# A two-layer graph network on one core: another order of the seven products of each block multiplication, of GpSimd's work and of the matrix M, and another prologue

## The chip, the cores and the metric

The kernel runs on one core of a Trainium2 chip. The core has five engines that run their own instruction queues side by side: TensorE (PE in the profile, its weight loads PEld), VectorE (DVE), ScalarE (ACT), GpSimd (POOL) and SyncE (SP), which here issues all DMA transfers. The metric is the device time of one execution in microseconds (us), lower is better. Three runs of the kernel before gave 2621.05, 2624.15 and 2624.7 us; the median is 2624.15 us.

## The reference

There are 128 graphs of 128 nodes, with x of 128x128x512 and an adjacency of 128x128x128, all float32. Two layers follow each other, each behind a layer norm and a relu and each added to its input. Cut to what matters:

```
# layer 0
h = maximum(layernorm(x), 0)
A_hat = adj + eye;  d = A_hat.sum(-1) ** -0.5
x = x + (A_hat * d[:, :, None] * d[:, None, :]) @ (h @ W0 + b0)

# layer 1
h  = maximum(layernorm(x), 0)
H  = (adj != 0);  Dn = 1 / (H @ adj[:, 0, :]);  Be = 1 / H.sum(axis=1)
conv(z, W, b) = Dn * (H @ (Be * (H^T @ (z @ W^T)))) + b
r  = layernorm(relu(conv(h, W1, b1))) * gamma + beta     # 1024 wide
x  = x + conv(r, W2, b2)
```

## The kernel before, in words

Two graphs form a pair, two pairs a group of four graphs. There are 64 pairs and 32 groups. The weights stay in SBUF. For each group the kernel forms, from the adjacency, the transposed matrix for layer 0 (`aT`), H transposed (`hT`), the same scaled by Be (`hb`, L237, on GpSimd) and M = H Be H^T (`m`, four 128-wide products at L245 in `adj_M`), so that layer 1 needs one product with M per convolution.

**Three block multiplications per pair.** The products with W0 (`s_w0`), W1 (`s_w1`) and W2 (`s_w2`) go through `strassen` (L342 on): rows are split by the two graphs of the pair, columns and the inner size in halves, so that seven products of blocks stand where eight would be. The products are called after their left and right blocks: 11·11, 12·21, s1·t1, s2·t2, s3·t3, 22·t4, s4·22. The left sums s1 to s4 are made in `left_sums` (L331 to L334, four GpSimd instructions in a chain) for W0 and W2, in `left_matmul` (L278 to L281) for W1. The right sums t1 to t4 are made once per weight in `Weight.sums` (L81). Results leave PSUM through VectorE or ScalarE, and two of the seven combinations per multiplication run on GpSimd (L376, u4, and L379).

**The stages.** The work is a software pipeline written out by hand (`tc.manual_schedule()`): the instructions of an engine run in the order in which the program gives them. In stage t, TensorE does W1 of pair t, then, if t is even, M of the next group, then W2 of pair t-1, W0 of pair t+2, and then four short things: the last product with M (`s_kv`, L519), the two products with M ahead of W1 (`s_mhT`, L458), the product with `aT` (`s_lap`, L422), and, if t is odd, the four transposes of `adj_T` (L220). There are 65 stages, t = 0 to 64.

**Filling.** Work of VectorE that is not tied to a product (statistics, edges, normalisation) stands in a list, `fill`, with a cost for each item. After each product `fill.give` adds the spare time of that product to an account and emits items from the front of the list while the account covers them; `fill.all` empties the list. A GpSimd instruction that an item emits takes its place in GpSimd's queue at that moment.

**The chain of pair t in its stage.** W1's result `r` is scaled and shifted (`first`, L478, one 128x1024 instruction per graph, i = 1 and then 0), put through relu on ScalarE (L481), its statistics are taken (`second`, L484 and L486), `chain` (L160 to L170) makes 1/std and the shift out of them, `norm2` (L499, two GpSimd instructions) applies them, and `turn` (L287) transposes 32x32 blocks on VectorE. At the stage's end `s_zT` issues 16 transfers (L324) that finish the transposition, into the tile `na`, the left blocks of W2 in the next stage. The same holds for pair t+3 and W0: `start` (L394) makes `h0` from x, `turn` follows, and `s_h0T` issues 16 transfers into `la`. The tile `r` has one buffer, so that the next stage's W1 can write its result only once the 16 transfers have read it.

The order in stage t is

```
W1 of t with left_sums(na of t-1) ahead of it; base(t); stats_r, statistics -> list
left_sums(la of t+2);  [t even: adj_M];  W2 of t-1;  W0 of t+2;  fill.all()
s_zT(t);  s_h0T(t+3);  s_kv(t-1);  s_mhT(t+1);  s_lap(t+2);  [t odd: adj_T, loads]
```

`base` (L449 and L450) is four GpSimd additions that add b2 and the layer's input to the tile into which the result goes.

Of the kernel before, what the change touches and what calls it, by code (L numbers as in the profile page):

```python
# [14 lines left out]
P = 128  # L15
# [5 lines left out]
def adj_preln_kernel(  # L21
# [41 lines left out]
    class Weight:  # L63
# [11 lines left out]
        def sums(self, *which):  # L75

            b = self.b
            for k in which or range(4):
                t, x, y = (("t1", "12", "11"), ("t3", "22", "12"), ("t2", "22", "t1"), ("t4", "t2", "21"))[k]
                eng = nc.gpsimd if k == 3 else nc.vector  # L80
                eng.tensor_tensor(b[t], b[x], b[y], ALU.subtract)  # L81

    wt0 = Weight("w0", NF // 2, F // 2)
# [39 lines left out]
    def load_group(g):  # L123
        gs = slice(g * G, (g + 1) * G)
        a4 = load.tile([P, G, P], F32, tag="a4", name="a4")
        w4 = load.tile([P, G, P], F32, tag="w4", name="w4")
        x4 = load.tile([P, G, F], F32, tag="x4", name="x4")
        xs = x[gs].rearrange("g i f -> i g f")
        if g == 0:

            nc.sync.dma_start(x4[:, 0, :], xs[:, 0, :])
            nc.sync.dma_start(x4[:, 1, :], xs[:, 1, :])
            nc.sync.dma_start(a4, adj[gs].rearrange("g i j -> i g j"))
            nc.sync.dma_start(x4[:, 2, :], xs[:, 2, :])
            nc.sync.dma_start(x4[:, 3, :], xs[:, 3, :])
            weight0()
            nc.sync.dma_start(w4, adj[gs, 0, :].partition_broadcast(P))
        else:
            nc.sync.dma_start(a4, adj[gs].rearrange("g i j -> i g j"))
            nc.sync.dma_start(w4, adj[gs, 0, :].partition_broadcast(P))  # L140
            nc.sync.dma_start(x4, xs)
        groups[g] = {"x": x4, "a": a4, "w": w4}

# [68 lines left out]
    def adj_T(g):  # L214

        q = groups[g]
        a4, d = q["a"], q["d"]
        tr = psum.tile([P, G, P], F32, tag="ps", name="tr")
        for k in range(G):
            nc.tensor.transpose(tr[:, k, :], a4[:, k, :], ident)  # L220
        aT = prep.tile([P, G, P], F32, tag="aT", name="aT")
        nc.vector.tensor_tensor(
            aT, tr, ident.unsqueeze(1).to_broadcast([P, G, P]), ALU.add
        )
        hT = prep.tile([P, G, P], F32, tag="hT", name="hT", bufs=1)
        nc.vector.tensor_scalar(hT, tr, 0.0, None, ALU.not_equal)
        nc.gpsimd.tensor_tensor(aT, aT, d.unsqueeze(2).to_broadcast([P, G, P]), ALU.mult)
        bi = small.tile([P, G], F32, tag="bi", name="bi")
        hb = prep.tile([P, G, P], F32, tag="hb", name="hb", bufs=1)
        q.update(aT=aT, hT=hT, hb=hb)  # L230

        def first():

            nc.vector.tensor_reduce(bi, hT, AX.X, ALU.add)
            nc.vector.tensor_scalar_max(bi, bi, 1.0)
            nc.vector.reciprocal(bi, bi)
            nc.gpsimd.tensor_tensor(hb, hT, bi.unsqueeze(2).to_broadcast([P, G, P]), ALU.mult)  # L237

        fill.add(1000, first)
# [105 lines left out]
    def strassen(a, wt, tag, dst, bias=None):  # L345


        h = wt.half

        def tmp(n):  # L350
            return work.tile([P, h], F32, tag=n, name=tag + n, bufs=1)


        pe, add = wt.nk * h * 1.68, 70 + h * 1.21

        def taken(n, ps, k):
            t = tmp(n)
            if bias is None:
                nc.scalar.copy(t, ps)
                fill.give(pe)  # L360
            else:
                nc.vector.tensor_tensor(t, ps, bias[:, k, :], ALU.add)
                fill.give(pe - add)
            return t

        def summed(t, a, b, op=ALU.add):
            nc.vector.tensor_tensor(t, a, b, op)  # L367
            return t

        u1 = taken("u1", product(a, wt, "11", "11"), 0)  # L370
        summed(dst[0][0], product(a, wt, "12", "21"), u1)
        fill.give(pe - add)
        u5 = taken("u5", product(a, wt, "s1", "t1"), 1)
        u2 = summed(tmp("u2"), product(a, wt, "s2", "t2"), u1)
        u4 = tmp("u4")
        nc.gpsimd.tensor_tensor(u4, u2, u5, ALU.add)  # L376
        fill.give(pe - add)
        u3 = summed(tmp("u3"), product(a, wt, "s3", "t3"), u2)
        nc.gpsimd.tensor_tensor(dst[1][1], u3, u5, ALU.add)  # L379
        fill.give(pe - add)  # L380
        summed(dst[1][0], u3, product(a, wt, "22", "t4"), ALU.subtract)
        fill.give(pe - add)
        summed(dst[0][1], product(a, wt, "s4", "22"), u4)
        fill.give(pe - add)

    def start(t):

        c = pairs[t] = {}
        c["q"], c["k"] = groups[t // 2], (t % 2) * 2
        q = c["q"]  # L390
        h = work.tile([P, 2, F], F32, tag="h0", name="h0", bufs=1)
        for i in range(2):
            k = c["k"] + i
            nc.scalar.activation(  # L394
                h[:, i, :], q["x"][:, k, :], AF.Relu,
                bias=q["nb"][:, k : k + 1], scale=q["s"][:, k : k + 1],
            )
        c["h0"] = h

        if t > 2:  # L400
            for i in range(2):
                fill.add(610, turn, h[:, i, :])
# [67 lines left out]
    def stats_r(mv, t):  # L470
# [15 lines left out]
                nc.vector.bn_aggr(mv[:, R + i, :], st[:, i].rearrange("p j s -> p (j s)"))  # L486

        for i in (1, 0):
            fill.add(1290, first, i)
        for i in (1, 0):  # L490
            fill.add(680, second, i, 0)
            fill.add(880, second, i, 1)
# [68 lines left out]
    def weight1():  # L561

        rows = [w[:, n, :] for w in s["w1"] for n in range(w.shape[1])]
        for r, w in enumerate(rows):
# [4 lines left out]
            for k in range(2):  # L569
# [1 line left out]
                    wt1.b[f"{k + 1}{j + 1}"][:, :, n * P : (n + 1) * P],  # L571
                    ps[:, 2 * k : 2 * k + 2, :],
                )
        wt1.sums()

    def weight2():

        rows = [w[:, n, :] for w in s["w2"] for n in range(w.shape[1])]
        for r, w in enumerate(rows):
            j, n = divmod(r, NF // 2)  # L580
            for k in range(2):
# [4 lines left out]
                for c in range(4):  # L586
                    nc.tensor.transpose(ps[:, c, :], wk[:, c // 2, c % 2], ident)
                nc.scalar.copy(wt2.b[f"{k + 1}{j + 1}"][:, :, n * P : (n + 1) * P], ps)
        bb = work.tile([P, NH, P], F32, tag="na", name="bb", bufs=1)
        nc.vector.tensor_copy(bb, be_col.unsqueeze(2).to_broadcast([P, NH, P]))  # L590
        pc = psum.tile([P, F], F32, tag="ps", name="pc")
        for c in range(NH):
            for j in range(2):
# [8 lines left out]
    def weight2_sums():  # L602
        def scaled(k, j):
            g = g_col[:, 4 * k : 4 * k + 4].unsqueeze(2).to_broadcast([P, 4, F // 2])
            b = wt2.b[f"{k + 1}{j + 1}"]
            nc.vector.tensor_tensor(b, b, g, ALU.mult)

        for k in range(2):
            for j in range(2):
                fill.add(1290, scaled, k, j)  # L610
        for k in range(4):
            fill.add(1290 if k < 3 else 0, wt2.sums, k)

# [3 lines left out]

    s = {}  # L620

    def statistics(t, lo, g):

        mv = s["mv"]

        def done(sc, nb):
            if g is not None:
                groups[g].update(s=sc[:, X : X + G], nb=nb[:, X : X + G], d=sc[:, D : D + G])
            fill.add(1300, lambda: None)
            if has(t + 3):  # L630
                start(t + 3)
            if has(t + 1):
                norm1(t + 1, sc, nb)
            if has(t):
                norm2(t, sc, nb)

        chain(mv, lo, D + G if g is not None else X1 + 2 if has(t + 1) else X1, done)

    def new_mv():
        s["mv"] = small.tile([P, 12, 2], F32, tag="mv", name="mv")  # L640
# [1 line left out]

    with tc.manual_schedule():
        load_group(0)
        load_group(1)
        load_weight1()
        stats_x(new_mv(), 0)
        statistics(-3, X, 0)
        fill.all()
        s_h0T(0)  # L650
        left_sums(pairs[0]["a0"])
        wt0.sums()
        nc.vector.tensor_tensor(b0_bc[:, 1, :], b0_bc[:, 1, :], b0_bc[:, 0, :], ALU.subtract)
        start(1)
        fill.all()
        s_h0T(1)
        adj_T(0)
        edges(0)
        s_w0(0)
        fill.all()  # L660
        adj_M(0)
        s_lap(0)
        stats_x1(new_mv(), 0)
        stats_x(s["mv"], 1)
        weight1()
        load_weight2()
        left_sums(pairs[1]["a0"])
        s_w0(1)
        statistics(-1, X1, 1)
        fill.all()  # L670
        s_h0T(2)
        s_lap(1)
        s_mhT(0)
        adj_T(1)
        load_group(2)
        for t in range(NP + 1):
            g = (t + 3) // 2
            odd = t % 2 == 1 and has(t + 3)
# [3 lines left out]
                stats_x1(s["mv"], t + 1)  # L682
            if odd:
                stats_x(s["mv"], g)
            if even:
                edges(g)
            if has(t - 1):
                left_sums(pairs[t - 1]["a2"])
            if has(t):
                s_w1(t)  # L690
                base(t)
                stats_r(s["mv"], t)
                statistics(t, R, g if odd else None)
            if has(t + 2):
                left_sums(pairs[t + 2]["a0"])
            if even:
                adj_M(g)
            if has(t - 1):
                s_w2(t - 1)
            if t == 0:  # L700
                fill.all()
                weight2()
            if has(t + 2):
                s_w0(t + 2)
            fill.all()
            if has(t):
                s_zT(t)
            if has(t + 3):
# [4 lines left out]
                s_mhT(t + 1)  # L713
            if has(t + 2):
                s_lap(t + 2)
            if t == 0:
                weight2_sums()
            if odd:
                adj_T(g)
                if has(t + 5):  # L720
                    load_group((t + 5) // 2)


# [25 lines left out]
```

## Time and profile before

| | |
|---|---|
| three runs, median | 2624.15 us |
| the profiled execution, its time | 2626.01 us |
| the profiled execution, its span (first to last instruction) | 2624.2 us |
| TensorE busy | 2415.7 us, 92% of the span |
| VectorE busy | 1915.0 us, 73% |
| GpSimd busy | 1611.5 us, 61% |
| ScalarE busy | 505.0 us, 19% |
| mean granted TensorE clock | 0.966 of full speed |

The span is what the lines of the profile add up to; the 1.8 us between the span and the execution's own time lie outside the first and the last instruction. TensorE's instructions overlap (their ends are modelled), so the distance from one start to the next tells more than a row's duration. A float32 product of blocks appears as several rows: each matmul of the program is two of the profile. The chain that ended last lies on TensorE for 62% of the span, on SyncE's queue for 11%, on VectorE for 10% and on GpSimd for 8%.

### The profile page before, as it was taken

The numbers are of one execution on the slowest core, as the hardware profiler recorded it, in microseconds if no ns is written. First come the engines' busy times: TensorE is split into PE (matmuls) and PEld (weight loads), VectorE is DVE, ScalarE is ACT, GpSimd is POOL, SyncE is SP. The second block draws the span as 40 slices with busy tenths as digits, with TensorE's granted clock in tenths as the row PEclk, the third lists the DMA queues.
The fourth block names the chain that finished last, engine by engine and source line by source line (L and its number), as shares of the span: only waits on it lengthen the run. The fifth ranks groups of instructions, "written<-read, shape, count | busy, mean of one in ns | idle before, by whom it ended". The sixth has DMA issues, their size and how long they took to land.

```text
span 2624.2 us, 31135 instructions
## 1 busy us (share of the span) xinstructions
PE 2415.7 (92%) x9208; PEld 1717.6 (65%) x9208; DVE 1915.0 (73%) x3671; ACT 505.0 (19%) x769; POOL 1611.5 (61%) x1481
## 2 busy tenths in 40 slices
PE   5789999999999999999999999999999999999996
PEld 4566676676676676676666776666766666766764
DVE  5667777787787786787777777777777777777863
ACT  2121121221121221221221221211211211211210
POOL 2646566566566576575675675665665665665663
PEclk8989999999999999999999999999999999999998
DMA  5124334333334333334333334333334333333222
GB/s 168 25 59 81 59 72 85 76 72 70 68 71 88 74 72 71 67 72 87 70 78 57 78 76 80 73 81 56 76 79 78 73 82 56 75 80 77 49 52 57
DMA packets 492615, 191.42 MB, mean 73 GB/s; under 512 B 423968, under 2 KB 457760, under 8 KB 492448
## 3 DMA queue, kind: packets, MB, share of 16 engines
q1 hardware_dynamic: 492448, 189.42, 35.4%
q8 instruction: 77, 1.26, 0.2%
q14 instruction: 90, 0.74, 0.1%
HBM read 56.63 MB, written 33.55 MB: 34 GB/s over the span
## 4 chain that ended last, share of the span: by engine, by line
PE 62%; SPq 11%; DVE 10%; POOL 8%; issue 5%; DMA 3%; ACT 1%; DVEq 0%; POOLq 0%; ACTq 0%
PE py L339 52%; SPq L324 11%; PE po L519 3%; PE m L458 3%; PE po L422 2%; PE mp L245 2%; POOL ns L333 2%; DVE st L484 2%; POOL ns L332 2%; POOL ns L331 2%; DMA na<-r 2%; DVE r L478 2%; POOL hb L237 1%; DVE r L287 1%; DVE y L367 1%
## 5 line engine op out<-in xcount | busy, mean ns | idle before, releaser
L367 DVE TENSOR_TENSOR r<-py,fu 128x512 f32<-128x512 f32 x128 | 88.3, 690 | 401.1 <-DMA na<-r 195.0
L331 POOL TENSOR_TENSOR ns<-na 128x512 f32<-128x512 f32 x64 | 81.3, 1270 | 468.4 <-DMA na<-r 271.9
L339 PE MATMUL py<-w2t,ns 128*128 128x256 f32 x1536 | 342.2, 379 | 0.6 <-DVE w2t L81 0.6
L339 PE MATMUL py<-w1t,ms 128*128 128x512 f32 x768 | 340.0, 592 | 0.0
L339 PEld LDWEIGHTS py<-w2t,ns 128*128 128x128 f32 x1536 | 301.2, 196 | 31.2 <-issue 1.0
L339 PE MATMUL py<-w,na 128*128 128x256 f32 x1024 | 273.0, 427 | 12.0 <-DMA na<-r 12.0
L339 PEld LDWEIGHTS py<-w,na 128*128 128x128 f32 x1024 | 229.0, 227 | 60.0 <-issue 23.9
L339 PEld LDWEIGHTS py<-w1t,ms 128*128 128x128 f32 x768 | 145.9, 190 | 183.7 <-issue 176.0
L478 DVE SCALAR_TENSOR_TENSOR r<-r,di,b_bc 128x1024 f32<-128x1024 f32 x128 | 257.0, 2008 | 6.7 <-POOL r L379 6.7
L481 ACT ACTIVATE r<-r 128x1024 f32<-128x1024 f32 x128 | 135.4, 1058 | 637.5 <-DVE r L478 449.4
L339 PE MATMUL py<-w,ma 128*128 128x512 f32 x512 | 230.3, 592 | 0.0
L450 POOL TENSOR_TENSOR x<-x,h 128x512 f32<-128x512 f32 x128 | 218.2, 1705 | 10.0
L449 POOL TENSOR_TENSOR x<-x,b_bc 128x512 f32<-128x512 f32 x128 | 202.0, 1578 | 0.0
L280 POOL TENSOR_TENSOR ms<-ms,ma 128x256 f32<-128x256 f32 x64 | 46.6, 728 | 241.5 <-DVE ms L278 241.5
L499 POOL TENSOR_SCALAR r<-r,s,nb 128x1024 f32<-128x1024 f32 x128 | 152.1, 1199 | 56.6 <-DVE nb L170 56.6
L339 PE MATMUL py<-w0t,ls 128*128 128x256 f32 x768 | 178.3, 382 | 6.4 <-POOL ls L331 6.4
L179 DVE BATCH_NORM_STATS2 st<-x 128x6 f32<-128x512 f32 x256 | 172.1, 672 | 5.7 <-DMA x<-in_x 5.7
L484 DVE BATCH_NORM_STATS2 st<-r 128x6 f32<-128x512 f32 x256 | 171.4, 670 | 0.0
L245 PE MATMUL mp<-hT,hb 128*128 128x128 f32 x256 | 54.9, 381 | 125.8 <-POOL hb L237 125.8
L339 PEld LDWEIGHTS py<-w0t,ls 128*128 128x128 f32 x768 | 151.8, 198 | 22.5 <-POOL ls L331 6.8
L339 PEld LDWEIGHTS py<-w,ma 128*128 128x128 f32 x512 | 94.8, 190 | 107.2 <-issue 106.9
L287 DVE STREAM_TRANSPOSE r<-r 128x1024 f32<-128x1024 f32 x128 | 158.0, 1237 | 3.1 <-POOL r L499 3.1
(126 smaller groups left out, 4518.1 us busy)
## 6 DMA issues: line engine op xcount, KB each, us to landing
na<-r SPq DMA_DIRECT2D x1024, 64.0 KB, 2.1
out<-o SPq DMA_DIRECT2D x128, 256.0 KB, 2.3
x<-in_x SPq DMA_DIRECT2D x31, 1024.0 KB, 10.5
la<-h SPq DMA_DIRECT2D x976, 32.0 KB, 1.9
a<-in_adj SPq DMA_DIRECT2D x32, 256.0 KB, 3.2
w<-in_adj SPq DMA_DIRECT2D x32, 256.0 KB, 8.6
x<-in_x SPq DMA_DIRECT2D x4, 256.0 KB, 4.1
w1a<-in_L_gnn_W SPq DMA_DIRECT2D x1, 1024.0 KB, 13.7
```

Of the source, the lines that this page charges most:

```text
L179: nc.vector.bn_stats(st, x)
L287: nc.vector.transpose(x, x)
L324: nc.sync.dma_start(Av[32 * m : 32 * m + 32, :, n, :], xv[32 * n : 32 * n + 32, :, m, :])
L331: nc.gpsimd.tensor_tensor(f["s1"], f["21"], f["22"], ALU.add)
L339: nc.tensor.matmul(ps[:, : wt.half], a.block(la, c), wt.b[lb][:, c, :], start=(c == 0), stop=(c == wt.nk - 1),)
L367: nc.vector.tensor_tensor(t, a, b, op)
L449: nc.gpsimd.tensor_tensor(xi, xi, b2_bc, ALU.add)
L450: nc.gpsimd.tensor_tensor(xi, xi, c["h1"][:, i, :], ALU.add)
L478: nc.vector.scalar_tensor_tensor(r[:, i], r[:, i], q["di"][:, k0 + i : k0 + i + 1], b1_bc, ALU.mult, ALU.add)
L481: nc.scalar.activation(r[:, i], r[:, i], AF.Relu)
L484: nc.vector.bn_stats(st[:, i, j, :], c["r"][:, i, j, :])
L499: nc.gpsimd.tensor_scalar(ri, ri, s[:, R + i : R + i + 1], nb[:, R + i : R + i + 1], ALU.mult, ALU.add)
```

## The change

1. **Order of the seven products** (in `strassen`): 12·21 moves from the second place to the last, so s1·t1 follows 11·11 at once.
2. **Order in the stage**: `left_sums` of `na` moves from ahead of W1 to behind it, after a `fill.all()` that is new there. `adj_M` and `left_sums` of `la` move from ahead of W2 to behind it, right ahead of W0.
3. **1/std of x**: `statistics` is split into `chain_group` (x of a group) and `chain_pairs` (r and x1). In odd stages the chain of x is put into the list ahead of W1, and pair t+3's `start` behind it; in even stages `start(t + 3)` is called ahead of W1. So `h0` is made and turned during W1; it has two buffers in place of one.
4. **Fill costs**: `first` of `stats_r` is booked at 1800 in place of 1290.
5. **Loads and buffers**: the first row of the adjacency (`w4`) is loaded by `load_edges`, behind x and with one buffer; `aT` has one buffer in place of two.
6. **Prologue and first stages**: x of group 1 and the left sums of pair 1 are taken earlier, `wt1.sums()` later, the wide copy of beta (`bb`) earlier (`beta_wide`); the right sum t4 of W2 moves from GpSimd to VectorE, and the sums of W2's blocks are listed ahead of W0 of stage 0.

```diff
@@ strassen
         u1 = taken("u1", product(a, wt, "11", "11"), 0)
-        summed(dst[0][0], product(a, wt, "12", "21"), u1)
-        fill.give(pe - add)
         u5 = taken("u5", product(a, wt, "s1", "t1"), 1)
...
         summed(dst[0][1], product(a, wt, "s4", "22"), u4)
         fill.give(pe - add)
+        summed(dst[0][0], product(a, wt, "12", "21"), u1)
+        fill.give(pe - add)
@@ start
-        h = work.tile([P, 2, F], F32, tag="h0", name="h0", bufs=1)
+        h = work.tile([P, 2, F], F32, tag="h0", name="h0", bufs=2)
@@ stats_r
-            fill.add(1290, first, i)
+            fill.add(1800, first, i)
@@ adj_T
-        aT = prep.tile([P, G, P], F32, tag="aT", name="aT")
+        aT = prep.tile([P, G, P], F32, tag="aT", name="aT", bufs=1)
@@ Weight.sums
-                eng = nc.gpsimd if k == 3 else nc.vector
+                eng = nc.gpsimd if k == 3 and self is not wt2 else nc.vector
@@ load_group, and new beside it
-            nc.sync.dma_start(w4, adj[gs, 0, :].partition_broadcast(P))
...
+    def load_edges(g):
+        gs = slice(g * G, (g + 1) * G)
+        w4 = groups[g]["w"] = load.tile([P, G, P], F32, tag="w4", name="w4", bufs=1)
+        nc.sync.dma_start(w4, adj[gs, 0, :].partition_broadcast(P))
@@ in place of statistics
+    def chain_group(g, then=None):
+        def done(sc, nb):
+            groups[g].update(s=sc[:, X : X + G], nb=nb[:, X : X + G], d=sc[:, D : D + G])
+            if then is not None:
+                start(then)
+        chain(s["mv"], X, D + G, done)
+
+    def chain_pairs(t):
+        def done(sc, nb):
+            fill.add(1300, lambda: None)
+            if has(t + 1):
+                norm1(t + 1, sc, nb)
+            if has(t):
+                norm2(t, sc, nb)
+        chain(s["mv"], R if has(t) else X1, X1 + 2 if has(t + 1) else X1, done)
@@ the stages
             if odd:
                 stats_x(s["mv"], g)
+                chain_group(g, t + 3)
+            elif has(t + 3):
+                start(t + 3)
             if even:
                 edges(g)
+            if has(t):
+                s_w1(t)
+            fill.all()
             if has(t - 1):
                 left_sums(pairs[t - 1]["a2"])
             if has(t):
-                s_w1(t)
                 base(t)
                 stats_r(s["mv"], t)
-                statistics(t, R, g if odd else None)
-            if has(t + 2):
-                left_sums(pairs[t + 2]["a0"])
-            if even:
-                adj_M(g)
+                chain_pairs(t)
             if has(t - 1):
                 s_w2(t - 1)
             if t == 0:
                 fill.all()
                 weight2()
+                weight2_sums()
+            if even:
+                adj_M(g)
             if has(t + 2):
+                left_sums(pairs[t + 2]["a0"])
                 s_w0(t + 2)
-            fill.all()
+            if t:
+                fill.all()
```

The order that the changed program has in an odd stage, between W1 and the end of W0, is on VectorE: 11·11's and s1·t1's result of W2, `first` of graph 1, s2·t2's result, `first` of graph 0, s3·t3's result, the statistics with three more results between them, the chain, then W0's results with the two turns of r among them. On GpSimd it is: the two combinations of W1, the four left sums of `na`, the four additions of `base`, the two combinations of W2, the two instructions of `norm2`, the four left sums of `la`, the two combinations of W0. In an even stage the order is the same, and TensorE has M between W2 and W0.

## The prediction

> **What bounds the kernel now.** I read the page first, then the waits of TensorE, its timeline over two stages with the granted clock, and GpSimd's and VectorE's timelines over the same stages.
>
> ```profile
> PE 2415.7 (92%) x9208; PEld 1717.6 (65%) x9208; DVE 1915.0 (73%) x3671; ACT 505.0 (19%) x769; POOL 1611.5 (61%) x1481
> ```
>
> TensorE is the bound; whatever leaves it busy is nearly free. Its waits:
>
> ```profile
> PE mp L245 <- POOL hb L237: 125.8, 30, 5.1
> PE pt L311 <- ACT h L394: 19.8, 3, 12.2
> PE po L422 <- DVE y L367: 14.2, 29, 1.6
> ```
>
> One wait recurs: M (L245) waits 30 times for `hb`, once in two stages. Its place, in TensorE's timeline (start and duration in us):
>
> ```profile
> 1344.34 3.60 PE L339 MATMUL py<-w,ma 128*128 128x512 f32 x8
> ...
> 1354.64 1.88 PE L339 MATMUL py<-w,ms 128*128 128x512 f32 x4
> 1360.63 1.44 PE L245 MATMUL mp<-hT,hb 128*128 128x128 f32 x8 [4.10 <-POOL hb L237]
> 1361.86 5.06 PE L339 MATMUL py<-w,na 128*128 128x256 f32 x16
> 1366.76 5.34 PE L339 MATMUL py<-w2t,ns 128*128 128x256 f32 x24
> ...
> 1375.39 1.89 PE L339 MATMUL py<-w,la 128*128 128x256 f32 x8
> ...
> 1381.43 1.88 PE L519 MATMUL po<-y,m 128*128 128x512 f32 x4
> ...
> 1386.65 3.60 PE L339 MATMUL py<-w,ma 128*128 128x512 f32 x8
> ...
> 1398.67 3.62 PE L339 MATMUL py<-w,na 128*128 128x256 f32 x16
> ```
>
> The even stage goes from 1344.34 to 1386.65, 42.31. W1's last product starts at 1354.64 and takes 1.72 (start to start in the rows around it), so TensorE stands from 1356.36 to 1360.63, 4.27. Then it is slow: 1.23 for M, where M took 0.89 without a wait (71.84 to 72.73), and 4.90 for two products of W2, which take 3.45 in the odd stage. The windows show why; the third number from the right, the granted TensorE clock, is 0.70 of full speed over the stretch behind the wait and 1.00 after it:
>
> ```profile
> 1361.80:1366.70 4.90, 4.90 (x18) 4.15 (x17) 2.25 (x4) 0.58 (x1) 4.82 (x5) 0.70 0.71 195
> 1366.70:1371.90 5.20, 5.20 (x26) 4.73 (x25) 5.20 (x7) 2.12 (x2) 5.04 (x5) 1.00 0.50 100
> ```
>
> So a wait of 4.27 costs 4.27+0.34+1.45 = 6.06. The 30 such waits, all of about 4 and longer, lost 1.5 to 2.9 to the clock, mostly 1.8. Without it: W1 12.02 (1386.65 to 1398.67), W2 12.08, W0 6.05 (1375.39 to 1381.43), the four short things 5.22 without, 5.66 with the transposes (0.44). That is 35.37 per stage, 36.25 with M, 35.81 with the transposes. Stage 2's W1 starts at 154.13 and stage 62's at 2527.84: 2373.71 for 30 pairs of stages, 79.12 a pair, against 72.06 at full rate.
>
> **What is removed.** `adj_M` goes behind W2, 12.08 later. `hb` comes late now because it stands on GpSimd behind four left sums that wait for the 16 transfers:
>
> ```profile
> 1354.06 1.28 POOL L331 TENSOR_TENSOR ns<-na 128x512 f32<-128x512 f32 x1 [7.02 <-DMA la<-h]
> ...
> 1359.53 1.04 POOL L237 TENSOR_TENSOR hb<-hT,bi 128x512 f32<-128x512 f32 x1
> ```
>
> Its input was ready at 1347.6. Changed, it runs ahead of these sums, 20 us before M wants it. All of 6.06 a pair goes, and the 0.5 of L422, whose last input now has the 3.5 of L519 and L458 as cover.
>
> **What is added.** `left_sums` of `la` is issued behind `norm2` on GpSimd, and the second product of W0 is now s1·t1. So TensorE waits in W0 for chain, `norm2` and a sum. Now these sums run early, at 1369.00; `norm2` comes later:
>
> ```profile
> 1369.00 1.71 POOL L331 TENSOR_TENSOR ls<-la 128x256 f32<-128x256 f32 x1
> ...
> 1375.70 2.39 POOL L499 TENSOR_SCALAR r<-r,s,nb 128x1024 f32<-128x1024 f32 x2 [1.44 <-DVE nb L170]
> ```
>
> VectorE's side, in the same stage:
>
> ```profile
> 1365.57 2.33 DVE L478 SCALAR_TENSOR_TENSOR r<-r,di,b_bc 128x1024 f32<-128x1024 f32 x1
> ...
> 1375.36 0.16 DVE L170 SCALAR_TENSOR_TENSOR nb<-mv,s 128x4 f32<-128x4 f32 x1
> ```
>
> Changed, counted from W1's start: W2 starts at 12.02; `first` follows the result of W2's second product (at 1800 booked, two gives of 1340 are needed), 3.45+0.42 later; from `first` to `norm2` is 10.13 now (1365.57 to 1375.70), with the two `first`, four statistics, five results and the short chain of four columns, the same in number afterwards; `norm2` 2.39; the first sum 0.73 (its row in the odd stage, 1409.24) with hand-over 0.75. The sum s1 is there at 12.02+3.87+10.13+2.39+0.75 = 29.16. TensorE wants it after W2 and one product of W0: 12.02+12.08+0.86 = 24.96 in an odd stage, 25.84 with M. It waits 4.2 and 3.3. The odd stage now has `norm2` 15.1 after W2's start, with a chain of twelve columns (1411.17 to 1413.59, against 1.0 for four); the split takes 1.4 of that off, and 13.8 stays, so the walk agrees with it. Uncertain: 0.7 either way, by the spread of rows (0.73 to 1.71 for one sum).
>
> What comes behind: six products of W0, 5.19, and 5.22 or 5.66. With 1.8 of slow clock after each wait, the even stage is 29.16+5.19+5.22+1.8 = 41.37, the odd 41.81; a pair 83.18, 4.06 more than now. Thirty pairs: +122.
>
> The shorter wait is the doubtful one, as no recurring wait of that length occurs. One of 2.95 in the prologue (ahead of 148.42) was followed by 2.50 and 2.78 for rows that take 1.79 and 1.72, a loss of 1.77; one of 2.46 near the end (2554.57) by none. I take 3.3 with the loss, since it is nearer to 2.95; without it in even stages a pair is 81.38. The Trainium skill, "TensorE: Matmul & The Clock Gate", Part 1, says that the clock halves after an idle window of about 3.4 us and that windows run free of the kernel. By it 3.3 would mostly pass unpunished and the time would be some 54 lower; the 2.95 above speaks against it.
>
> **What costs nothing, and its cover.** `left_sums` of `na` behind W1: its transfers landed at 8.1 and 9.7 after W1's start, W1's GpSimd combinations end at 9.3, s1 is there at 10.6, wanted at 12.02+1.72 = 13.74; the cover is 3.1, and beyond it TensorE waits one for one. `base` (6.6) then ends near 21.3 and W2's u4 at 22, wanted by VectorE near 23; behind it would stand the statistics and the chain, so a delay beyond 1 lengthens the new wait. Turns of r end some 7.5 after s1, so SP starts the 16 transfers then (10.4 of issue) and lands them 7.4 into the next stage; GpSimd's first write to `r` is at 7.6, thin but with the 3.1 behind it. SP's next 16 (`la`, 11.1) land 18 in, wanted from 24. Loads of x and `w4` follow them; `w4`'s one buffer makes SP wait for `edges`, done by 13. The second chain of odd stages (1.6) and the turns of `h0` lie in VectorE's 6.5 idle of W1. `aT`'s buffer is free once L422 has read it, which comes earlier in TensorE's order. VectorE's load does not grow, but for t4.
>
> **Prologue.** The left sums of pair 1 come before W0 of pair 1: its gap (33.29 to 39.83, 6.5) and slow clock (2.1) go. The gap of 6.3 and 1.6 before 54.31 shrinks by some 6, for x's statistics are earlier; wt1's sums cover what remains. W2's wait at 77 to 86 stays, since its copies stand behind ScalarE's work on r. t4 takes 1.7 on VectorE (row of the other sums) in place of a wait of 5.1, but delays `first` in stage 1. I take -16, between -25 (both gaps and that wait) and +5 (VectorE late in stage 1). The tail, without W0, stays.
>
> **Sum.** Span 2624.2+122-16 = 2730; with the 1.8 around it 2732; the profiled execution is 1.9 above the median of the runs, so 2730.
>
> **Rivals.**
> A. The clock falls in odd stages alone: 2730-54 = 2676. For it: 3.3 is shorter than all recurring waits. Against: the 2.95.
> B. No clock loss, or s1 earlier by 1.8: a pair costs what it costs now, less the prologue: about 2620. It decides from s1 at 27.4 with the loss, 29.2 without it.
> C. Faster: no wait in W0, since TensorE is never ahead of s1. Then a pair is 72.06, and 2624-212-16 = 2396. It decides from s1 at 25, by 4.2 earlier than walked; for it speaks that VectorE is idle for 2.65 ahead of W2's first result now (before 1365.23). Against it: `norm2` alone starts 13.84 and 15.10 after W2's start, so 25.9 and 27.1 in these terms, and GpSimd runs in order.
> D. A longer wait: GpSimd's `base`, between both left sums, delays W2's u4 by over 1, VectorE and the chain behind it. 1 more a stage and up to 0.5 more of clock is +90: 2820.
> E. M still waits for `hb` behind W2: then 2730 would hold too, since M ends ahead of s1.
>
> **Chances.** The forecast 0.57 (with E), A 0.20, B 0.08, C 0.05, D 0.10. Own range of the forecast 2690 to 2775. The range, with A and part of D, is 2640 to 2800; B, C and half of D stay out. About 0.2% is what can be told from no change here: faster 0.09 (C and half of B), the same 0.03, slower 0.88.
>
> **What would show it.** The waits of L245 for L237 vanish; in their place stand some 62 waits of L339 (`ls`) for GpSimd L333 of the changed program, 3 to 4.5 each; PEclk falls in W0, not W2; `norm2` ends ahead of them on GpSimd; stages are near 41.6. Wrong, if the second product of W0 starts 0.86 after the first.

## The result, and the profile after

The changed kernel takes 2803.65 us (median of 4 runs, 2803.54 to 2803.78) against 2624.28 us of the kernel before on the same chip: ratio 1.0686, 95% interval 1.0668 to 1.0705. It is slower by 6.9%, and 74 us slower than predicted. Most lines of the changed program that are named here are shifted by two (L339 is now L341).

The page's busy times, its group of W0's products, and TensorE's largest wait (total, times, longest):

```profile
PE 2475.0 (88%) x9208; PEld 1747.2 (62%) x9208; DVE 2011.1 (72%) x3858; ACT 512.4 (18%) x800; POOL 1580.9 (56%) x1480
...
L341 PE MATMUL py<-w0t,ls 128*128 128x256 f32 x768 | 303.1, 574 | 274.0 <-POOL ls L333 274.0
```

```profile
PE py L341 <- POOL ls L333: 274.0, 61, 11.0
```

M has no wait for `hb` any more, and L424 none for `y`. One wait recurs in their place, 61 times: W0's second product waits for the first left sum of `la`. TensorE's timeline, an odd stage and the next even one, with the wait in brackets (from the end of a product at full rate, 0.86, the gaps are 5.67 and 3.15):

```profile
1384.82 1.88 PE L341 MATMUL py<-w,ma 128*128 128x512 f32 x4
...
1408.93 1.03 PE L341 MATMUL py<-w,la 128*128 128x256 f32 x4
1415.46 5.23 PE L341 MATMUL py<-w0t,ls 128*128 128x256 f32 x12 [5.51 <-POOL ls L333]
1420.53 1.03 PE L341 MATMUL py<-w0t,la 128*128 128x256 f32 x4
...
1428.78 1.88 PE L341 MATMUL py<-w,ma 128*128 128x512 f32 x4
...
1452.88 1.05 PE L247 MATMUL mp<-hT,hb 128*128 128x128 f32 x8
1453.77 1.03 PE L341 MATMUL py<-w,la 128*128 128x256 f32 x4
1457.78 4.54 PE L341 MATMUL py<-w0t,ls 128*128 128x256 f32 x12 [2.97 <-POOL ls L333]
1462.16 1.03 PE L341 MATMUL py<-w0t,la 128*128 128x256 f32 x4
```

The three products behind the wait take 5.07 us in the odd stage (1415.46 to 1420.53) and 4.38 in the even one; at full rate 2.59. The windows give the granted clock in the third column from the right, first for each wait and then for what follows it:

```profile
1409.90:1415.40 5.50, 0.05 (x1) 0.00 (x0) 2.40 (x10) 1.72 (x3) 3.05 (x3) 0.82 0.00 0
1415.40:1420.50 5.10, 5.04 (x12) 4.06 (x13) 1.64 (x3) 0.00 (x0) 2.81 (x5) 0.52 0.01 3
1454.70:1457.70 3.00, 0.11 (x1) 0.00 (x0) 0.42 (x1) 1.90 (x3) 3.00 (x3) 1.00 0.20 29
1457.70:1462.10 4.40, 4.32 (x12) 3.58 (x13) 1.03 (x3) 0.00 (x0) 2.21 (x5) 0.61 0.00 0
```

What TensorE waits for, on GpSimd, in the odd stage:

```profile
1405.80 1.70 POOL L376 TENSOR_TENSOR gu<-gu,gu 128x256 f32<-128x256 f32 x1 [1.50 <-DVE gu L369]
1407.46 0.73 POOL L379 TENSOR_TENSOR y<-gu,gu 128x256 f32<-128x256 f32 x1
1412.35 2.37 POOL L501 TENSOR_SCALAR r<-r,s,nb 128x1024 f32<-128x1024 f32 x2 [4.16 <-DVE nb L172]
1414.69 0.72 POOL L333 TENSOR_TENSOR ls<-la 128x256 f32<-128x256 f32 x1
```

GpSimd stands idle for 4.16 us until r's chain is done, does `norm2`, and only then the sum, whose data were there since 1402.85, when the last transfer into `la` landed. Where the time went, by the starts of W1:

| | before | predicted | after |
|---|---|---|---|
| start of stage 2 | 154.13 | 138 | 145.78 |
| even stage, mean of 30 | 42.61 | 41.37 | 41.23 |
| odd stage, mean of 30 | 36.52 | 41.81 | 44.10 |
| pair of stages | 79.12 | 83.18 | 85.33 |
| from stage 62 to the end | 96.36 | 96.36 | 96.08 |

-8.35 for the prologue, 30 times 6.21 for the pairs and -0.3 for the tail make +177.6, which is the difference of the spans (2801.8 and 2624.2).

### The profile page after: what moved, and what is told of

The parts are those of the page before. It is cut to its first block, busy times and chain, and to the rows that moved or that the text cites. A ratio compares the mean times of both kernels' runs of the same rounds, so it can differ in the third digit from the quotient of the medians.

```text
span 2801.8 us, 31328 instructions
## 1 busy us (share of the span) xinstructions
PE 2475.0 (88%) x9208; PEld 1747.2 (62%) x9208; DVE 2011.1 (72%) x3858; ACT 512.4 (18%) x800; POOL 1580.9 (56%) x1480
## 4 chain that ended last, share of the span: by engine, by line
PE 42%; DVE 19%; POOL 12%; SPq 12%; issue 7%; DMA 6%; ACT 1%; POOLq 0%; DVEq 0%; ACTq 0%
PE py L341 33%; SPq L326 12%; DMA w<-in_adj 4%; DVE r L480 3%; DVE st L486 3%; PE po L521 3%; POOL r L501 3%; PE m L460 2%; PE po L424 2%; POOL x L451 2%; POOL x L452 2%; DVE y L369 2%; POOL ls L333 2%; DVE s L171 1%; DVE u L170 1%
## 5 line engine op out<-in xcount | busy, mean ns | idle before, releaser
L341 PE MATMUL py<-w0t,ls 128*128 128x256 f32 x768 | 303.1, 574 | 274.0 <-POOL ls L333 274.0
L341 PEld LDWEIGHTS py<-w0t,ls 128*128 128x128 f32 x768 | 226.7, 304 | 347.5 <-POOL ls L333 298.2
L341 PE MATMUL py<-w2t,ns 128*128 128x256 f32 x1536 | 342.7, 380 | 0.5 <-POOL ns L333 0.5
L341 PE MATMUL py<-w1t,ms 128*128 128x512 f32 x768 | 340.5, 592 | 1.9 <-DVE w1t L81 1.2
L341 PEld LDWEIGHTS py<-w2t,ns 128*128 128x128 f32 x1536 | 301.8, 197 | 31.5 <-POOL ns L333 0.9
L364 DVE TENSOR_TENSOR eu<-py,b_bc 128x256 f32<-128x256 f32 x128 | 54.1, 423 | 311.5 <-POOL ls L336 276.3
L341 PEld LDWEIGHTS py<-w1t,ms 128*128 128x128 f32 x768 | 145.7, 190 | 186.6 <-issue 169.0
L341 PE MATMUL py<-w,na 128*128 128x256 f32 x1024 | 243.8, 381 | 15.1 <-DMA na<-r 14.6
L341 PEld LDWEIGHTS py<-w,na 128*128 128x128 f32 x1024 | 201.7, 197 | 64.5 <-issue 40.9
L341 PE MATMUL py<-w,ma 128*128 128x512 f32 x512 | 240.8, 592 | 0.0
L480 DVE SCALAR_TENSOR_TENSOR r<-r,di,b_bc 128x1024 f32<-128x1024 f32 x128 | 235.6, 1842 | 0.0
L376 POOL TENSOR_TENSOR fu<-fu,fu 128x512 f32<-128x512 f32 x64 | 82.0, 1281 | 241.2 <-DVE fu L369 241.2
L452 POOL TENSOR_TENSOR x<-x,h 128x512 f32<-128x512 f32 x128 | 192.6, 1505 | 10.0
L274 ACT COPY ma<-m 128x512 f32<-128x512 f32 x64 | 37.5, 586 | 712.0 <-PE m L460 712.0
L341 PEld LDWEIGHTS py<-w,ma 128*128 128x128 f32 x512 | 94.8, 190 | 107.2 <-issue 105.9
```

Source lines behind the costliest of these rows:

```text
L341: nc.tensor.matmul(ps[:, : wt.half], a.block(la, c), wt.b[lb][:, c, :], start=(c == 0), stop=(c == wt.nk - 1),)
L452: nc.gpsimd.tensor_tensor(xi, xi, c["h1"][:, i, :], ALU.add)
L480: nc.vector.scalar_tensor_tensor(r[:, i], r[:, i], q["di"][:, k0 + i : k0 + i + 1], b1_bc, ALU.mult, ALU.add)
```

## The experiments

All times stand beside runs of the kernel before on the same chip (medians 2623.6 to 2626.5).

**The sums for W0 ahead of W2's products, all else as changed.**

```
             if has(t - 1):
+                if has(t + 2):
+                    left_sums(pairs[t + 2]["a0"])
                 s_w2(t - 1)
...
             if has(t + 2):
-                left_sums(pairs[t + 2]["a0"])
                 s_w0(t + 2)
```

> The changed kernel, with the left sums of la issued ahead of W2, behind base, as before the change. Theory (TensorE waits in W0 because these sums stand behind norm2 on GpSimd): both waits of a pair of stages (3.1 and 6.1 us) and the slow clock behind them (1.8 and 2.2) go; a pair of stages takes 72 to 73 us in place of 85.3, the kernel 2385 to 2440 us. The wait of 11 us in stage 1 goes too. Rival (the statistics, the chain and VectorE are simply too late for this order, so that the wait moves to the next reader: the left sums of na, or M, or L422): above 2560 us, with a recurring wait of TensorE at another line.

2458.33 us, ratio 0.9369 (0.9353 to 0.9385), a little over the expected band. The pair takes 74.03 us, 11.3 less than in the changed kernel, and the granted clock is 0.992 over the span (0.937 in the changed kernel). No wait for `ls` is left. One other wait recurs, about once in two stages:

```profile
PE po L424 <- DVE y L369: 45.6, 36, 2.0
```

So the place of four sums in GpSimd's order turns the change from 6.3% faster than before into 6.9% slower. This version beats both kernels.

**x's chain behind r's chain**, in the changed kernel: `chain_group` of odd stages is called after `chain_pairs`. What hangs on it, the scaling to `h0` and `h0`'s two turns, moves with it.

> The changed kernel, with the chain of x in odd stages put into the list behind the chain of r. Theory (the odd stage's wait is 6.1 us and not 4.2 because the chain of x runs on VectorE beside GpSimd's left sums of na, at 1.2 us for an instruction that takes 0.17 with GpSimd idle, and delays the first scaling of r to 18.4 us after W1's start): the first scaling starts 15.9 after W1's start, the odd wait falls to 4 to 4.5 us, the even one stays at 3.1 to 4, the kernel takes 2730 to 2775 us. Rival (the odd stage is late because of the four statistics of x, which stay in W1): the odd wait stays near 6, the kernel near 2800.

2762.56 us (median of two runs), ratio 1.0525 (1.0504 to 1.0546), as expected. The odd stage, W1 from 1446.07 on:

```profile
1462.18 1.81 DVE L480 SCALAR_TENSOR_TENSOR r<-r,di,b_bc 128x1024 f32<-128x1024 f32 x1
```

```profile
1474.95 4.55 PE L341 MATMUL py<-w0t,ls 128*128 128x256 f32 x12 [3.76 <-POOL ls L333]
```

`first` starts 16.1 us after W1's start, and the odd stage takes 41.61 on the mean of 30, close to the predicted 41.81. In the changed kernel `first` starts 18.44 after it (1403.26), 18.7 on the mean. So x's chain with the turns of `h0` behind it, in W1, is what lengthened odd stages, and not the statistics of x, which stayed in W1. The run doesn't part the chain from the turns, but in even stages the turns of `h0` lie in W1 as well, and `first` starts at 16.1 there. The even stage rises to 42.55, so only half of the gain is kept: GpSimd's write to `r` waits 1.49 us for `na`'s transfers there, its additions of `base` come later, and VectorE waits 1.76 for W2's combination behind them. What takes the time in W1 is seen in the changed kernel's VectorE timeline:

```profile
1396.76 1.19 DVE L170 TENSOR_TENSOR u<-u,y 128x8 f32<-128x8 f32 x1
1397.98 1.19 DVE L171 SCALAR_TENSOR_TENSOR s<-u,y 128x8 f32<-128x8 f32 x1
1399.20 1.19 DVE L172 SCALAR_TENSOR_TENSOR nb<-mv,s 128x4 f32<-128x4 f32 x1
...
1403.26 2.13 DVE L480 SCALAR_TENSOR_TENSOR r<-r,di,b_bc 128x1024 f32<-128x1024 f32 x1
```

These instructions of eight and four columns take 1.19 us each, where r's chain of four columns takes 0.16 an instruction with GpSimd idle (1411.42 to 1412.17). With x's chain moved, the instructions of L170 and L171 on the same eight columns run with GpSimd idle, at 1477.12 and 1477.32, and take 0.17 each. In the changed kernel GpSimd at the same time adds up `na` and begins `base`:

```profile
1396.66 1.26 POOL L335 TENSOR_TENSOR ns<-na 128x512 f32<-128x512 f32 x1
1397.88 1.26 POOL L336 TENSOR_TENSOR ns<-na,ns 128x512 f32<-128x512 f32 x1
1399.10 1.27 POOL L451 TENSOR_TENSOR x<-x,b_bc 128x512 f32<-128x512 f32 x1
```

Each small instruction ends when one of GpSimd's ends (1397.95 beside 1397.92, 1399.17 beside 1399.14, 1400.39 beside 1400.37).

**Small instructions beside GpSimd, by themselves.** `two`, `one` and `both` are six tensor_tensor, tensor_scalar and scalar_tensor_tensor each on 8 columns of SBUF, `out_of_psum` six tensor_tensor with one operand in PSUM; three parts, the second beside 24 additions of 128x512 on GpSimd (lines L72 to L86).

```
+        part(None, 0)
+        part(pool_two, 24)
+        part(pool_one, 24)
```

> A kernel of its own, that computes nothing of the reference and writes one small tile: VectorE's instructions of 8 columns (two SBUF operands; one operand with a scalar; scalar_tensor_tensor of two SBUF operands; one operand out of PSUM and one of SBUF), six of each, first with GpSimd idle, then beside GpSimd's additions of 128x512, then beside GpSimd's tensor_scalar of 128x512. Theory: some 0.17 us each with GpSimd idle; beside the additions those with two SBUF operands end when an instruction of GpSimd ends, so 1.2 us each, while those with one SBUF operand stay under 0.25. Rival: the small instructions of odd stages were slow for another reason (each depends on the one ahead of it): then all take the same with and without GpSimd.

The four groups with GpSimd idle, then beside its additions (start, duration of six), in one execution:

```profile
4.64 1.16 DVE L72 TENSOR_TENSOR dv<-dv 128x8 f32<-128x8 f32 x6
5.84 1.20 DVE L76 TENSOR_SCALAR dv<-dv 128x8 f32<-128x8 f32 x6
7.07 1.17 DVE L80 SCALAR_TENSOR_TENSOR dv<-dv 128x8 f32<-128x8 f32 x6
8.28 1.17 DVE L86 TENSOR_TENSOR dv<-pt,dv 128x8 f32<-128x8 f32 x6
...
9.88 4.16 DVE L72 TENSOR_TENSOR dv<-dv 128x8 f32<-128x8 f32 x6
14.07 4.03 DVE L76 TENSOR_SCALAR dv<-dv 128x8 f32<-128x8 f32 x6
18.13 4.02 DVE L80 SCALAR_TENSOR_TENSOR dv<-dv 128x8 f32<-128x8 f32 x6
22.19 1.17 DVE L86 TENSOR_TENSOR dv<-pt,dv 128x8 f32<-128x8 f32 x6
```

The size is GpSimd's doing: with all operands in SBUF, 1.16 to 1.20 us for six become 4.0 to 4.2. Two details were expected otherwise. One by one, every second instruction takes 1.1 to 1.27 us and its neighbour 0.16 to 0.17, so it is not one wait for each (here none reads the result of the one ahead, as the chain's do). And the one-operand form waits as well; only the form with a PSUM operand runs free, 1.17 for six. Beside GpSimd's tensor_scalar the SBUF forms take 2.1 to 2.2 for six. The Trainium skill, "SBUF — State Buffer", section "Who interferes with whom", says that VectorE and GpSimd share one pair of ports, held for a whole instruction by whichever is first while the other stands still. These rows agree: 1.27 is the length of one addition on GpSimd, and the long instructions end 0.02 to 0.03 us after such an addition.

**The clock after waits of growing length.** Blocks of 48 products, and between two blocks a wait for VectorE (`cols` columns):

```
+        for cols in (0, 512, 768, 1024, 1280, 1536, 1792, 2048, 2560, 3072, 4096, 6144):
+            gap(ps, cols)
+            ps = block(48)
```

> A kernel of its own, that computes nothing of the reference: TensorE does blocks of 48 products of 128x512 f32, and between two blocks it waits for two small instructions of VectorE and one of growing length; the waits grow from some 0.6 to some 7 us. A block at full clock takes 48 times 0.43 = 20.6 us. Theory, from the stages of the changed kernel: no loss up to 2.5 us, from some 3.0 us on the block is longer by 1.8 us, and by about 2.4 us behind 6 us. Rival, the Trainium skill's idle window of some 3.4 us (TensorE: Matmul & The Clock Gate, Part 1): waits of 3.0 to 3.3 us cost nothing here either, and what fell behind them in the changed kernel fell for another reason.

One product of 512 columns in f32 is two records of 0.43 us here, so a block at full clock takes 41.47 and not the 20.6 of the expectation. TensorE's timeline, block by block:

```profile
185.62 41.47 PE L70 MATMUL pb<-b,a 128*128 128x512 f32 x96 [1.72 <-DVE a L78]
229.08 43.16 PE L70 MATMUL pb<-b,a 128*128 128x512 f32 x96 [1.99 <-DVE a L78]
274.50 41.47 PE L70 MATMUL pb<-b,a 128*128 128x512 f32 x96 [2.26 <-DVE a L78]
318.48 43.00 PE L70 MATMUL pb<-b,a 128*128 128x512 f32 x96 [2.52 <-DVE a L78]
364.36 41.44 PE L70 MATMUL pb<-b,a 128*128 128x512 f32 x96 [2.88 <-DVE a L78]
409.21 43.13 PE L70 MATMUL pb<-b,a 128*128 128x512 f32 x96 [3.41 <-DVE a L78]
456.30 44.05 PE L70 MATMUL pb<-b,a 128*128 128x512 f32 x96 [3.95 <-DVE a L78]
...
555.91 43.73 PE L70 MATMUL pb<-b,a 128*128 128x512 f32 x96 [7.15 <-DVE a L78]
```

Neither expectation holds. A wait of 1.99 or 2.52 costs 1.7 and 1.5 us of clock (granted 0.76 and 0.77 over the next 7 us, against 1.00 behind 2.26 and 2.88), while 2.26 and 2.88 cost nothing; from 3.41 on all four do, with 1.7 to 2.6 (the block behind 5.01, not shown, lost 1.94). Between 2 and 2.9 us the length of a wait does not say whether the clock falls. The Trainium skill's "TensorE: Matmul & The Clock Gate" (Part 1) has the clock halve after an idle window of about 3.4 us, in windows that run free of the kernel. Free windows fit the mixed answers; but a wait of 1.99 holds no idle window of 3.4, so the measurement differs from the page there. In the changed kernel all 30 even waits, 2.9 to 3.2 us long, lost clock, 1.8 on the mean; why none of them was spared is open. Two of the versions below show mixed answers in the whole kernel too.

**M behind W2 alone, in the kernel before.**

> The kernel before, with adj_M behind W2 and nothing else changed. Theory of the prediction (a wait of 6.06 us a pair goes): 2624 - 182 = 2442 us. Rival (a loop of its own bounds the stage then: transfers into na, left sums of na, W1's two GpSimd combinations behind them, scaling, statistics, chain, norm2, turn, transfers again, about 38 us from landing to landing in the odd stage of the profile): stages of about 38 us, the kernel at 2520 to 2550, and the wait of TensorE at W2's sums or at L422.

2549.79 us, ratio 0.9715 (0.97 to 0.9729), the rival's upper end. M's wait goes, 6.06 a pair, but the pair falls by 2.53 only, to 76.59: behind it L422 waits for `y`, 51 times and 83.9 us in all (14.2 before), since r's turn stands ahead of `y` on VectorE (in the stage of the longest such wait, 1222.84 to 1224.00). Taking M's wait away does not give full rate.

**The order of the products**: 12·21 second again, in the changed kernel, and in the version with the early sums.

```
         u1 = taken("u1", product(a, wt, "11", "11"), 0)
+        summed(dst[0][0], product(a, wt, "12", "21"), u1)
+        fill.give(pe - add)
...
-        summed(dst[0][0], product(a, wt, "12", "21"), u1)
-        fill.give(pe - add)
```

> The changed kernel, with 12.21 as the second of the seven products again. Theory: the sum s1 of W0 is ready at the same time (29.0 and 31.1 us after W1's start), but TensorE has one product more ahead of it, so that the waits fall by 0.86 us to 2.3 (even) and 5.2 (odd). If a wait of 2.3 is too short for the clock to fall, the even stage loses 1.8 more and the kernel takes about 2700 us; if the clock falls all the same, about 2750. Rival (the order of the products is the cause of the waits): the waits vanish, 2450 or less.

> GpSimd's sums for W0 ahead of W2's products, and the product 12 times 21 second again. Theory: the second result of W1 waits for the transfers that still read r (some 5 us on VectorE, hidden from TensorE in part), r's scaling and all behind it come some 4 us later, TensorE waits for s1 or for the transfers into na, and the pair of stages is 76 to 78.5 us against 74.03, so 2520 to 2600 us. Rival: with W0's wait gone the later r finds slack, and the time stays within 1% of 2458.

In the changed kernel: 2944.10 us, ratio 1.1212 (1.1193 to 1.123). With the early sums: 2712.64, ratio 1.0337 (1.0315 to 1.0358). Both are far above what either side of their expectations gave. For the second the mechanism was named and its price was too low; for the first it was not named, since s1 was taken to be ready at the same time. VectorE and TensorE in an even stage of the second version, W1 from 1210.60 on, and the same wait in an earlier even stage:

```profile
1220.28 0.69 DVE L369 TENSOR_TENSOR r<-py,fu 128x512 f32<-128x512 f32 x1 [6.37 <-DMA la<-h]
```

```profile
567.50 7.14 PE L341 MATMUL py<-w2t,ns 128*128 128x256 f32 x24 [2.33 <-POOL ns L333]
...
1228.57 5.45 PE L341 MATMUL py<-w2t,ns 128*128 128x256 f32 x24 [2.33 <-POOL ns L333]
```

With 12·21 second, W1's second result is the first write to `r`, and VectorE waits 6.37 us for the transfers that still read it (the profile names a transfer of `la`, in the same queue behind them). Everything of W1 comes later, GpSimd's combinations too; the left sums of `na` stand behind these, and W2's s1·t1 waits for them 60 times (139.6 us in all). With 12·21 last, the first write to `r` is GpSimd's, later in W1, and most of the transfers are through by then: VectorE's writes to `r` wait 82.8 us for transfers in all, and GpSimd's 131.7, where VectorE's wait 409.0 here. The pair is 8.45 us longer than with the changed order (82.48 against 74.03), and 4.36 longer in the changed kernel itself.

The two rows of TensorE also bear on the clock: the same wait of 2.33 us is followed by a granted clock of 0.76 over 7 us at 567.50 and of 1.00 at 1228.57. Of the 60 waits for `ns` in this run, 23 were followed by a lower clock, between 1.96 and 3.88 us long, and 37 were not, between 1.53 and 2.61.

**The left sums of `na` behind W1, in the kernel before with M moved.** The call of `left_sums` for `a2` goes behind `s_w1`.

> The kernel before with M behind W2 and GpSimd's sums for W2 behind its work for W1, all else as before. Theory: the loop that set the time with M moved alone (76.59 a pair) gets shorter since the work for W1 no longer stands behind the sums of na: pair 73.5 to 75.5, so 2460 to 2520 us. Rival: the second result of W1 still waits for r's transfers on VectorE, GpSimd's combinations for W1 with it, and the pair stays at 76 or above, 2530 to 2560 us.

2722.54 us, ratio 1.0373 (1.0355 to 1.039): slower by 173 than with M alone, against both expectations. W2 waits for `ns` 60 times, 152.4 us, for the same reason; four of these waits, of 3.0 us, kept the full clock. So two parts of the change belong together: with 12·21 second, the sums of `na` behind W1's combinations lose. What they gain with 12·21 last was not tried by itself.

**Better versions tried, on top of the early sums.** x's chain behind r's:

> Both single moves together: GpSimd's sums for W0 ahead of W2's products, and in odd stages x's chain (with the scaling to h0 and its two turns) behind r's chain. Theory: in odd stages r's scaling then starts some 16 us after W1's first product instead of 18.4, so y's results of W2 no longer wait behind the turns of r on VectorE, and the wait of 2.0 us a time ahead of the product with x of odd stages shrinks; pair of stages 72.1 to 73.5 us against 74.03 with the first move alone, so 2400 to 2440 us. Rival: VectorE is as full as before, and the turns of h0, now later, fall into W2 beside its seven results; then the pair stays at 74 or above and the time at 2455 or more.

2532.15 us, ratio 0.9648 (0.9631 to 0.9666), so the rival. TensorE's recurring waits:

```profile
PE po L424 <- DVE y L369: 50.4, 61, 1.2
PE py L341 <- DVE ms L280: 29.1, 31, 1.0
PE m L460 <- DVE eu L369: 17.1, 30, 1.0
```

The move that gained 41 us in the changed kernel costs 74 here. There, x's chain ran in the time in which TensorE stood in W0 (1476.65 to 1477.68). Here nobody stands: in the trace VectorE has no wait from x's chain in W0 of an odd stage (1198.21) into the next W1 (1215.69), a sum that W1 needs comes late (0.95 us of TensorE's wait in that stage), and the even stage grows from 36.6 to 39.2. This is read from the trace and not tried.

x's chain ahead of x1's statistics (their two adds lie between its halves), and then the two additions of `base` for the second graph behind W2, with the sums of `la` ahead of `base`; the last run has this split without the move of x's chain:

> GpSimd's sums for W0 ahead of W2's products, and in odd stages the statistics and the chain of x ahead of x1's statistics (which lie between the two halves of the chain). Theory: the chain's small instructions then mostly miss GpSimd's four sums of na, which run from some 11.3 us after W1's first product on; r's scaling starts near 17.5 us after it instead of 20.5, the wait of 1.3 us for y in odd stages goes, and the pair of stages is 72.3 to 73.3 us against 74.03, so 2405 to 2440 us. Rival: GpSimd's combinations for W1, at 6.3 to 7.5 and 10 to 11.3, still catch them, or the turns of h0 are what matters: then the time stays within 0.5% of 2458.

> As with GpSimd's sums for W0 ahead of W2's products and x's chain ahead of x1's statistics; on GpSimd the sums for W0 now also stand ahead of the additions to x1, and half of these come behind W2's combinations. Theory: with x's chain early, VectorE waits in W2 for GpSimd's combination (2.05 us in an odd stage, 3.4 in an even one), which stands behind the additions to x1; two of these are 2.5 us of GpSimd, so r's chain, norm2 and the turns come some 2 us sooner in both stages, the wait of 1.27 us for y ahead of the product with x goes, and the pair is 72.2 to 73.2 us, so 2400 to 2435 us. Rival: norm2 now meets the other half of the additions on GpSimd, and the time stays within 0.5% of 2460.

> The same split of the additions to x1, with x's chain where the changed kernel has it, behind x1's statistics. Theory: in odd stages r's scaling still starts 20.5 us after W1's first product, so VectorE and not GpSimd sets r's chain there and the wait of 1.27 us stays: 2445 to 2460 us. Rival: GpSimd alone was the limit, and the time falls to the same 2400 to 2435 us as with both.

2461.40 us (0.9375, 0.9359 to 0.939), 2628.81 (1.0022, 1.0012 to 1.0032) and 2650.91 (1.0111, 1.0096 to 1.0126): the rival for the first, neither side for the other two. In the odd stages of the first, `first` starts 18.0 us after W1's start instead of 20.5, but VectorE then waits 2.05 for GpSimd's combination in W2, and nothing is gained. The split was meant to mend that and made two new waits; from the first of the two split versions:

```profile
PE m L460 <- ACT h L441: 161.0, 63, 4.9
```

```profile
1274.56 1.73 POOL L333 TENSOR_TENSOR ls<-la 128x256 f32<-128x256 f32 x1 [3.31 <-DMA la<-h]
```

ScalarE may write the one buffer of `h1` only when `base` has read it, which is now late; and the sums of `la`, ahead of `base`, stand for 3.3 us until their transfers land. That these two are the whole loss was read in the trace and not tried.

The fill costs, the buffers of `aT` and `w4`, and the parts of the prologue were not changed back one by one.

## Why the prediction was right and wrong, step by step

- **M's wait goes: right.** No wait of M for `hb` is left. In the even stage shown M starts at 1452.88, while `hb` was written from 1431.77 on. It was not worth full rate by itself, as M moved alone shows.
- **The new wait, its place and its releaser: right.** 61 waits for the first sum of `la`, some 62 forecast, behind `norm2`. That this place is what costs more than the rest of the change gains is shown by the early sums (2803.65 to 2458.33).
- **The even stage: right.** s1 was walked to 29.16 us after W1's start and is used at 29.00 (1457.78); the gap is 3.1 for 3.3, the loss 1.79 for 1.8, the stage 41.23 for 41.37.
- **The odd stage: the step that failed.** "The second chain of odd stages (1.6) and the turns of `h0` lie in VectorE's 6.5 idle of W1" was costed at nothing. The last three instructions of that chain alone take 3.6 us, since GpSimd's sums of `na` run beside them. `first` starts 18.44 after W1's start where 15.9 was walked; from there to `norm2` it is 9.1 for 10.13, which hides a part of the delay; so in the stage shown s1 is used at 30.6, 1.5 later, and behind the longer wait the clock loses 2.5 (2.3 on the mean) instead of 1.8. With chain and turns moved out of W1, `first` starts at 16.1 and the odd stage takes 41.61. In the changed kernel it is 44.10 for 41.81: 30 times 2.29 is +69 of the 72 us by which the span exceeds 2730; the prologue adds 8, and the even stages take 4 off. The trace of before held two warnings. The idle time of 6.5 is that of the even stage's W1; in the odd stage, where the chain had to fit, it was 5.50, a wait for transfers ahead of 12·21's write to `r`, and the new order takes most of that wait away, idle time and all (on VectorE 13.9 us of 375.5 stay in the whole kernel). And in the odd stage the last instructions of the chain took 0.59 to 0.65 beside GpSimd, against 0.16 for r's chain in the even stage without it:

```profile
1394.78 0.69 DVE L367 TENSOR_TENSOR r<-py,fu 128x512 f32<-128x512 f32 x1 [5.50 <-DMA na<-r]
...
1411.64 0.59 DVE L168 TENSOR_TENSOR u<-u,y 128x12 f32<-128x12 f32 x1
...
1412.94 0.65 DVE L170 SCALAR_TENSOR_TENSOR nb<-mv,s 128x8 f32<-128x8 f32 x1
```

- **The clock: right for this kernel, in part by luck.** Rival A fell, since all even stages lost clock. The 3.3 was taken as a loss from one wait of 2.95; the other runs show that waits of 2 to 3 us go either way, so one wait was too little to decide from.
- **The prologue: mis-sized.** -8.35 for -16. Pair 1's W0 waits no longer ahead of W1(0), which starts at 45.85 instead of 59.82. Stage 0 gives 5.4 of that back (50.94 for 45.55). Stage 1 is as long as before (48.99 for 48.76): the waits in W2 and ahead of L458 are gone, but W0 loses 11 of wait and 2 of clock, since VectorE has W2's scaled weights and sums in front of the statistics and `first` starts 24.7 after W1's start (96.79 to 121.52). The text had this inside its range, as "VectorE late in stage 1", and chose too near the other end. With the early sums this wait goes, stage 1 takes 42.07, and stage 2 starts at 137.49, near the forecast 138; so this error comes from the place of the sums too.
- **Rivals.** D's time (2820) came near, its mechanism did not occur: in the odd stage GpSimd waits 1.50 for VectorE ahead of W2's u4, and VectorE waits for u4 only 5 times, 3.9 us in all. B fell with the clock. C, that TensorE never waits in W0, needs the sums at another place; then the pair is 74.03, still above 72.06, mostly because `y` is late by 1.3 in odd stages.

What stayed unpriced altogether is how far the parts depend on each other: the new order of the products is worth 4.4 to 8.5 us a pair here, because it covers the wait for `r`'s transfers, and without it the later sums of `na` lose.

## What to carry to other kernels

Work that is moved on an engine with an ordered queue inherits every wait of what it is put behind; ask what it could have run beside, as here, where four sums whose data were ready stood behind a normalisation. Price a small VectorE instruction on SBUF operands by the GpSimd instruction beside it and not by its own width. Test a saving again in the version in which you want it: the same move of x's chain gained 41 us in one and lost 74 in the other.

## What the runs showed of the hardware

- VectorE's instructions of 8 columns, all operands in SBUF, took 0.16 to 0.17 us with GpSimd idle and up to 1.27 beside GpSimd's additions of 1.27, with one operand too; with an operand in PSUM they took 0.17 in both cases, in one execution.
- After a wait of 1.99 us TensorE lost 1.69 us to a slower clock, after one of 2.88 nothing, after 3.41 and longer always, in one execution with twelve waits. In the kernel with the early sums and the old order of products, waits of 2.33 us were followed by a clock of 0.76 twice and of 1.00 twice.
